# The last token block of a graph layer: multiplication beside the squares, negated offset, early residual loads and two store queues

## The chip, the cores and the metric

One core of one Trainium2 chip. The metric is the device time of one execution in microseconds (us), smaller is better. All numbers below are from executions on the chip.

## The reference, cut to what matters

```python
# x: (128, 64, 768) float32, adj: (128, 64, 64); two layers l of the same form
h = maximum(layernorm(x), 0)
for l in range(2):
    ...                                              # attention from h, W_left, W_right and adj
    h_lin = einsum('bsh,oh->bso', h, W_lin[l]) + b_lin[l]
    ctx = matmul(attention, h_lin)
    h = relu((ctx - mean(ctx)) / (std(ctx) + 0.001) * ln_a[l] + ln_b[l])
return x + h
```

The change touches only the last token block of the last pass: there h_lin is projected, ctx is multiplied, its rows are normalised, scaled by a, shifted by b, clipped at zero, and added to x. In the inputs used here a is all ones and b is all zeros, but the kernel is written for any a and b.

## The kernel before

The 8192 rows are worked through in 16 blocks u of 512 rows. Each block has two halves r, and each half two tiles k of 128 x 768. In the last block (u = 15) the halves are projected one after the other, in fifteen steps of four matmuls each; `run(n)` carries out what was planned with `put(n, ...)` for a place n in that stream. After a projection step the result is read out of PSUM into `hl` by ScalarE and VectorE ("eviction"). When all parts of a half are there, `context` multiplies, and `finish` normalises:

```python
def residual(u, r):                       # asks for the x rows of one half
    XS[u, r] = [sp.tile([P, H], F32, name="xr", bufs=4) for _ in range(2)]
    for k in range(2):
        for h in range(PAIR):
            nc.sync.dma_start(XS[u, r][k][h * S:(h + 1) * S], x[u * NBB + batch(r, k, h)])

def finish(u, r):
    cx = context(u, r)                    # TensorE: two tiles in PSUM
    zs = [sp.tile([P, H], F32, name="z", bufs=4 if last else 3) for _ in range(2)]
    # ... ss, sd, rs
    for k in range(2):                    # ScalarE: sums of squares
        nc.scalar.activation(zs[k].rearrange(two, n=2), cx[k], AF.Square, accum_out=ss[:, k:k + 1])
    nc.scalar.activation(sd, ss, AF.Sqrt, bias=floor, scale=1.0 / (H - 1.0))

    def inverse():
        nc.vector.tensor_scalar_add(rs, sd, EPS_LN)
        nc.vector.reciprocal(rs, rs)

    def scaled(k):
        # ... (last layer)
        nc.vector.scalar_tensor_tensor(zs[k].rearrange(two, n=2), cx[k], rs[:, k:k + 1],
                                       rows["a"].rearrange(two, n=2), op0=ALU.mult, op1=ALU.mult)
        nc.gpsimd.tensor_add(zs[k], zs[k], rows["b"])
        # ...

    def done(k):
        # ... (last layer)
        xs = XS[u, r]
        nc.vector.scalar_tensor_tensor(xs[k], zs[k], 0.0, xs[k], op0=ALU.max, op1=ALU.add)
        for h in range(PAIR):
            nc.sync.dma_start(out[u * NBB + batch(r, k, h)], xs[k][h * S:(h + 1) * S])
        if k and (u < NB - 1 or r == 0):
            residual(u + r, 1 - r)        # asks for the rows of a later half
    return [inverse] + [lambda k=k: scaled(k) for k in range(2)] + [lambda k=k: done(k) for k in range(2)]

# ... the last block: after projection step i, `finish` of a half is begun,
# and its five pieces (inverse, scaled, scaled, done, done) get these places
linear(u, (0,), 0, {0: ((u - 1, 0), (12, 13, 15, 19, 21)),
                    11: ((u - 1, 1), (34, 35, 36, 42, 44))}, (1,))
linear(u, (1,), 30, {4: ((u, 0), (50, 51, 52, 56, 58))}, ())
for n in sorted(plan):
    run(n)
for f in finish(u, 1):
    f()
```

Every engine works off its own instructions in this order. So a piece of `finish` that has to wait holds up all evictions behind it on the same engine: in the profile of this kernel VectorE's addition of (15,0) waits 1.85 us for its rows, and the eviction of Z behind it starts at 2775.32, 3.65 us after TensorE was through with Z (2771.67).

Of the kernel before, what the change touches and what calls it, by code (L numbers as in the profile page):

```python
# [10 lines left out]
F32 = mybir.dt.float32  # L11
I32 = mybir.dt.int32
AF = mybir.ActivationFunctionType
ALU = mybir.AluOpType
# [3 lines left out]
def kernel(  # L18
# [24 lines left out]
    nc = tc.nc  # L43
    B, S, H = x.shape
    L = w_lin.shape[0]
    P = 128
    C = H // P
# [3 lines left out]
    PAIR = P // S  # L51
    Q = 4
    T = Q * P
    TH = T // 2
    NB = B * S // T
    assert L == 2 and PAIR == 2 and C == 3 * K2 and TH == D
    EPS_IN, EPS_LN, EPS_ATT = 1e-5, 1e-3, 1e-10
# [4 lines left out]
    big = ctx.enter_context(tc.tile_pool(name="big", bufs=2))  # L62
    stat = ctx.enter_context(tc.tile_pool(name="stat", bufs=4))
# [5 lines left out]
    NBB = T // S  # L69
# [7 lines left out]
    def put(slot, *fs):  # L77
        plan.setdefault(slot, []).extend(fs)
# [129 lines left out]
    floor = const.tile([P, 1], F32, name="floor")  # L208
# [4 lines left out]
    for h in range(PAIR):  # L213
        r = slice(h * S, (h + 1) * S)
# [287 lines left out]
    rows = {}  # L502
# [45 lines left out]
    def pass_two(l, aside):  # L548
        last = l == L - 1
        with tc.tile_pool(name=f"two{l}", bufs=2, reuse_waits="tile") as sp:  # L550
# [8 lines left out]
            def load(u):  # L559
                if (2, l, u) not in HT:  # L560
                    load_h(2, l, u)
                AT[u] = sp.tile([P, Q, S], F32, name="at", bufs=3)
                nc.sync.dma_start(AT[u], ATT[l][u])

            def context(u, r):


                hl, at = HL[u], AT[u]
                lo, hi = slice(0, S), slice(S, P)
                cx = [ps_aux.tile([P, 2, T], F32, name="aux") for _ in range(2)]  # L570
                for n in range(2):
                    for (j, k, i) in ((lo, 0, lo), (hi, 0, hi), (lo, 1, hi), (hi, 1, lo)):
                        q = r + 2 * k
                        m = n if j == lo else 1 - n
                        nc.tensor.matmul(cx[k][i, m, :HH], at[j, q, :], hl[j, q, m * HH:(m + 1) * HH],  # L575
                                         start=True, stop=True)
                return [c[:, :, :HH] for c in cx]

            def batch(r, k, h):
                return 4 * (h if k == 0 else 1 - h) + r + 2 * k  # L580

            XS = {}

            def residual(u, r):
                XS[u, r] = [sp.tile([P, H], F32, name="xr", bufs=4) for _ in range(2)]
                for k in range(2):
# [5 lines that stand above are left out]
                cx = context(u, r)  # L592
                zs = [sp.tile([P, H], F32, name="z", bufs=4 if last else 3) for _ in range(2)]
                if last and not u and not r:
                    residual(u, r)
                two = "p (n d) -> p n d"
                ss = stat.tile([P, 2], F32, name="ss")
                sd = stat.tile([P, 2], F32, name="sd1")
                rs = stat.tile([P, 2], F32, name="rs1")
# [10 lines that stand above are left out]
                    if last:  # L610
                        nc.vector.scalar_tensor_tensor(  # L611
                            zs[k].rearrange(two, n=2), cx[k], rs[:, k:k + 1],
                            rows["a"].rearrange(two, n=2), op0=ALU.mult, op1=ALU.mult)
                        nc.gpsimd.tensor_add(zs[k], zs[k], rows["b"])  # L614
                        return
                    if (u, r, k) == (NB - 1, 1, 1):
                        nc.vector.tensor_scalar_mul(zs[k].rearrange(two, n=2), cx[k], rs[:, k:k + 1])
                    else:
                        nc.scalar.activation(zs[k].rearrange(two, n=2), cx[k], AF.Copy, scale=rs[:, k:k + 1])
                    for h in range(PAIR):  # L620
                        nc.sync.dma_start(ROWS[u][batch(r, k, h)], zs[k][h * S:(h + 1) * S])

                def done(k):
                    if last:
                        xs = XS[u, r]
                        nc.vector.scalar_tensor_tensor(xs[k], zs[k], 0.0, xs[k], op0=ALU.max, op1=ALU.add)
                        for h in range(PAIR):
                            nc.sync.dma_start(out[u * NBB + batch(r, k, h)], xs[k][h * S:(h + 1) * S])
                        if k and (u < NB - 1 or r == 0):
                            residual(u + r, 1 - r)  # L630

                return [inverse] + [lambda k=k: scaled(k) for k in range(2)] + [lambda k=k: done(k) for k in range(2)]
# [33 lines left out]
            for u in range(NB):  # L666
                turn = not last and u >= NB - 2
                if u + 1 < NB:
                    load(u + 1)
                    put_all(9 if u else 15, affine(2, l, u + 1))  # L670
                    put_sums_t((2, l, u + 1), 15 if u else 21, 1, 0)
                    if turn:
                        load_rows(1, 0, sp)
                        put_all(10, transpose_rows(1, 0, sp), 2)
                    if u in aside:
                        aside[u]()
                    ends = {}
                    if u:
                        ends = {0: ((u - 1, 0), (6, 7, 8, 11, 12)), 7: ((u - 1, 1), (20, 21, 22, 30, 30))}
                    linear(u, (0, 1), 0, ends, (0, 1) if u + 2 < NB else (0,))  # L680
                    for n in sorted(plan):
                        plan[n - 30] = plan.pop(n)
                else:
                    if turn:
                        load_h(1, 1, 0)
                        put_all(28, affine(1, 1, 0), 3)
                        put_sums_t((1, 1, 0), 38, 2, 30)
                    linear(u, (0,), 0, {0: ((u - 1, 0), (12, 13, 15, 19, 21)),
                                        11: ((u - 1, 1), (34, 35, 36, 42, 44))}, (1,))
                    linear(u, (1,), 30, {4: ((u, 0), (50, 51, 52, 56, 58))}, ())  # L690
                    for n in sorted(plan):
                        run(n)
                    for f in finish(u, 1):
                        f()

    def one_aside(l):
# [46 lines left out]
```

## Time and profile before

| | before |
|---|---|
| median of 3 runs | 2791.11 us (2790.47 to 2792.8) |
| span of the profiled execution | 2791.6 us (2793.33 as the runs count it, more than any of them) |
| start of the last token block in it | 2740.0 us |
| from there to the first of the last two squares | 37.9 us |
| from the block's start to the end of the last addition | 46.8 us |
| from the block's start to the end of the span | 51.5 us |

I read every trace relative to the **start of the last block**, which is the first of the four matmuls of its first projection step (X). The rows of the page and of the chain are shown in the prediction; the columns of a chain line are start, length, and what filled it; those of a timeline line are start, length, engine, source line, operation, output and inputs with their shapes, count, and in brackets how long the engine had been idle and what ended that.

### The profile page before, as it was taken

To read this page: it belongs to the slowest core of one execution; us is meant where nothing else is said; L and a number is where in the kernel's file an instruction comes from. 1 tells how busy PE (TensorE), PEld (TensorE's weight loads), DVE (VectorE), ACT (ScalarE), POOL (GpSimd) and SP (SyncE) were. 2 spreads that over 40 slices of the span, in tenths; PEclk is the share of its full clock that TensorE was granted. 3 is DMA by queue.
4 is the path that set the end of the run, shared out by engine and by line. 5 is a ranking of instruction groups with operands and counts; after the bars stand their busy time and mean duration, and the time that the engine had idled before them with its cause. 6 is when DMAs were issued, how large, how long until landed. Compare 5 with 4: busy or idle time off the path is not lost.

```text
span 2791.6 us, 46094 instructions
## 1 busy us (share of the span) xinstructions
PE 2751.3 (99%) x18712; PEld 2340.8 (84%) x18712; DVE 1340.8 (48%) x2215; ACT 837.8 (30%) x1453; POOL 1191.5 (43%) x935
## 2 busy tenths in 40 slices
PE   7999999999999999999999999999999999999997
PEld 6888888888888888888788888888888888888885
DVE  6455545454444332332345444544444335666666
ACT  2122222222231244444521211222121214445443
POOL 3332343223322456556432344223222325887875
PEclk9999999999999999999999999999999999999999
DMA  5533443344332243343555433443344204555654
GB/s 165 152 83 74 108 111 77 74 97 121 79 74 76 84 140 110 113 149 106 149 134 128 116 78 74 97 120 79 74 92 120 62 25 146 167 167 159 184 162 125
DMA packets 234068, 310.80 MB, mean 111 GB/s; under 512 B 54144, under 2 KB 184448, under 8 KB 225664
## 3 DMA queue, kind: packets, MB, share of 16 engines
q1 hardware_dynamic: 233568, 307.06, 41.5%
q8 instruction: 149, 2.44, 0.4%
q10 hardware_dynamic: 288, 0.79, 0.1%
q14 instruction: 63, 0.52, 0.1%
HBM read 202.91 MB, written 104.86 MB: 110 GB/s over the span
## 4 chain that ended last, share of the span: by engine, by line
PE 95%; issue 1%; DVE 1%; POOL 1%; DMA 1%; ACT 1%; SPq 0%; DVEq 0%; ACTq 0%; POOLq 0%
PE X L369 23%; PE V L369 15%; PE X L648 12%; PE Y L369 12%; PE Z L369 8%; PE V L648 8%; PE Y L648 6%; PE aux L395 5%; PE Z L648 4%; PE aux L575 3%; POOL w_r L145 1%; DVE wm L409 0%; DMA x<-in_x_dram 0%; DMA w_r<-in_w_right_dram 0%; DMA w_l<-in_w_left_dram 0%
## 5 line engine op out<-in xcount | busy, mean ns | idle before, releaser
L145 POOL TENSOR_TENSOR ts<-ht 128x512 f32<-128x512 f32 x441 | 586.4, 1341 | 1232.2 <-DMA ht<-h 567.6
L190 ACT ACTIVATE m<-X 128x512 f32<-128x512 f32 x256 | 152.5, 596 | 1106.7 <-PE X L369 582.4
L145 POOL TENSOR_TENSOR ts<-ht,ts 128x512 f32<-128x512 f32 x189 | 249.3, 1327 | 154.7 <-PE X L648 76.9
L145 DVE TENSOR_TENSOR m<-m,V 128x512 f32<-128x512 f32 x256 | 174.2, 680 | 269.5 <-PE V L369 269.4
L145 DVE TENSOR_TENSOR m<-m,X 128x512 f32<-128x512 f32 x256 | 163.7, 681 | 248.7 <-PE X L369 248.0
L369 PE MATMUL X<-ts,w_l 128*128 128x256 f32 x1024 | 244.7, 382 | 3.8 <-DVE w_l L145 2.1
L648 PE MATMUL X<-w_n,ts 128*128 128x256 f32 x1024 | 244.0, 380 | 0.8 <-ACT hl L190 0.6
L369 PE MATMUL X<-ts,w_r 128*128 128x256 f32 x1024 | 241.9, 379 | 0.0
L145 DVE TENSOR_TENSOR m<-m,Z 128x512 f32<-128x512 f32 x128 | 87.9, 687 | 313.4 <-ACT m L190 254.8
L369 PEld LDWEIGHTS X<-ts,w_l 128*128 128x128 f32 x1024 | 193.0, 191 | 35.5 <-DVE m L145 3.1
L648 PEld LDWEIGHTS X<-w_n,ts 128*128 128x128 f32 x1024 | 191.7, 190 | 31.7 <-DVE hl L145 1.8
L369 PEld LDWEIGHTS X<-ts,w_r 128*128 128x128 f32 x1024 | 192.3, 190 | 28.7
L256 ACT ACTIVATE ht<-ht,b_col,a_col 128x512 f32<-128x512 f32 x192 | 143.5, 804 | 142.6 <-DMA ht<-h 142.6
L648 PE MATMUL Y<-w_n,ts 128*128 128x256 f32 x768 | 182.4, 379 | 0.0
L369 PE MATMUL Y<-ts,w_l 128*128 128x256 f32 x768 | 181.4, 379 | 0.0
L369 PE MATMUL Y<-ts,w_r 128*128 128x256 f32 x768 | 181.4, 379 | 0.0
L190 ACT ACTIVATE hl<-X 128x512 f32<-128x512 f32 (+1 forms) x136 | 77.8, 572 | 329.2 <-PE X L648 326.3
L369 PEld LDWEIGHTS Y<-ts,w_r 128*128 128x128 f32 x768 | 145.9, 190 | 19.8
L369 PEld LDWEIGHTS Y<-ts,w_l 128*128 128x128 f32 x768 | 145.9, 190 | 19.8
L648 PEld LDWEIGHTS Y<-w_n,ts 128*128 128x128 f32 x768 | 145.9, 190 | 19.8
L614 POOL TENSOR_TENSOR z<-z,b 128x768 f32<-128x768 f32 x64 | 115.7, 1822 | 94.4 <-DVE z L611 94.4
L145 DVE TENSOR_TENSOR hl<-hl,X 128x512 f32<-128x512 f32 (+1 forms) x136 | 83.1, 652 | 146.6 <-PE X L648 141.8
(106 smaller groups left out, 4682.7 us busy)
## 6 DMA issues: line engine op xcount, KB each, us to landing
ht<-h SPq DMA_DIRECT2D x63, 1536.0 KB, 7.3
h<-xb SPq DMA_DIRECT2D x124, 384.0 KB, 6.4
z<-z SPq DMA_DIRECT2D x128, 192.0 KB, 2.9
x<-z SPq DMA_DIRECT2D x128, 192.0 KB, 8.5
xr<-in_x_dram SPq DMA_DIRECT2D x128, 192.0 KB, 3.7
out_dram<-xr SPq DMA_DIRECT2D x128, 192.0 KB, 2.6
x<-in_x_dram SPq DMA_DIRECT2D x120, 192.0 KB, 8.7
adj<-in_adj_dram SPq DMA_DIRECT2D x64, 128.0 KB, 2.7
```

The costliest lines, as they stand in the source:

```text
L145: (eng.tensor_add if sign == "+" else eng.tensor_sub)(o, a, b)
L190: nc.scalar.activation(to(o), p, AF.Copy, scale=1.0 if sign == "+" else -1.0)
L256: nc.scalar.activation(ht, ht, AF.Relu, bias=cols[1][:, c:c + 1], scale=cols[0][:, c:c + 1])
L369: nc.tensor.matmul(p[:, g], w[ORDER[i][0]][:, c, g * P:(g + 1) * P], b()[t][:, c, :], start=(new and g == c == 0), stop=(c == K2 - 1), ski ...
L395: nc.tensor.matmul(p[h * S + e:h * S + e + 32, q, e:e + 96], ht[:, c, b * S + e:b * S + e + 32], mb[:, e:e + 96], start=(c == 0), stop=(c ...
L575: nc.tensor.matmul(cx[k][i, m, :HH], at[j, q, :], hl[j, q, m * HH:(m + 1) * HH], start=True, stop=True)
L614: nc.gpsimd.tensor_add(zs[k], zs[k], rows["b"])
L648: nc.tensor.matmul(p[:, n], b[t][:, c, r * P:(r + 1) * P], w[s][:, c, :], start=(i in FIRST and i not in PRELOAD and n == c == 0), stop=(c ...
```

## The change

The intent: let the end of the kernel run shorter than 50 us without touching TensorE's work.

1. The x rows of the last block are loaded early, in one go, into the place of a block that is free by then ("ht"), instead of into the four shared buffers that only come free as earlier rows are stored.
2. The places of the pieces move: the context of (14,1) and of (15,0) begins two steps earlier, and the additions of (15,0) go behind the last evictions.
3. The last half gets its own code. Clipping with the offset is rewritten: max(z + b, 0) + x = max(z, -b) + (x + b). So -b and x + b can be formed early on GpSimd, and VectorE multiplies ctx by a while ScalarE still forms the squares; after the squares there remain scale-and-max and one addition.
4. The stores of these rows go out on two queues, of SyncE and ScalarE.

```diff
+            def last_block(u):
+                rest = big.tile([P, C, T], F32, name="ht").rearrange("p c t -> p (c t)")
+                rows["-b"] = sp.tile([P, H], F32, name="nb", bufs=1)
+                for r in range(2):
+                    XS[u, r] = [rest[:, n * H:(n + 1) * H] for n in (2 * r, 2 * r + 1)]
+
+                def load(r):
+                    for k in range(2):
+                        for h in range(PAIR):
+                            nc.sync.dma_start(XS[u, r][k][h * S:(h + 1) * S], x[u * NBB + batch(r, k, h)])
+
+                put(1, lambda: load(1))
+                put(6, lambda: nc.gpsimd.tensor_scalar_mul(rows["-b"], rows["b"], -1.0))
+                put(20, lambda: load(0))
+                for xs, slot in zip(XS[u, 1], (22, 40)):
+                    put(slot, lambda xs=xs: nc.gpsimd.tensor_add(xs, xs, rows["b"]))
+
+            def finish_last(u, r):
+                ... (cx, zs, squares, xs, ss, rs)
+                for k in (1, 0):
+                    nc.scalar.activation(squares[:, k].rearrange(two, n=2), cx[k], AF.Square, accum_out=ss[k])
+                    nc.vector.tensor_tensor(zs[1 - k].rearrange(two, n=2), cx[1 - k],
+                                            rows["a"].rearrange(two, n=2), op=ALU.mult)
+                    nc.scalar.activation(rs[k], ss[k], AF.Sqrt, bias=floor, scale=1.0 / (H - 1.0))
+                for k in (1, 0):
+                    nc.vector.tensor_scalar_add(rs[k], rs[k], EPS_LN)
+                    nc.vector.reciprocal(rs[k], rs[k])
+                    nc.vector.scalar_tensor_tensor(zs[k], zs[k], rs[k], rows["-b"], op0=ALU.mult, op1=ALU.max)
+                    nc.vector.tensor_add(xs[k], xs[k], zs[k])
+                    for h, queue in enumerate((nc.sync, nc.scalar)):
+                        queue.dma_start(out[u * NBB + batch(r, k, h)], xs[k][h * S:(h + 1) * S])
+                return []
...
-                        if k and (u < NB - 1 or r == 0):
+                        if k and u + r < NB - 1:
                             residual(u + r, 1 - r)
...
-                    linear(u, (0,), 0, {0: ((u - 1, 0), (12, 13, 15, 19, 21)),
-                                        11: ((u - 1, 1), (34, 35, 36, 42, 44))}, (1,))
-                    linear(u, (1,), 30, {4: ((u, 0), (50, 51, 52, 56, 58))}, ())
+                        ends = ({0: ((u - 1, 0), (12, 13, 15, 19, 21)), 11: ((u - 1, 1), (34, 35, 36, 42, 44))},
+                                {4: ((u, 0), (50, 51, 52, 56, 58))})
+                    else:
+                        last_block(u)
+                        ends = ({0: ((u - 1, 0), (12, 13, 15, 19, 21)), 9: ((u - 1, 1), (28, 29, 30, 39, 41))},
+                                {2: ((u, 0), (44, 45, 47, 61, 62))})
+                    linear(u, (0,), 0, ends[0], (1,))
+                    linear(u, (1,), 30, ends[1], ())
                     for n in sorted(plan):
                         run(n)
-                    for f in finish(u, 1):
+                    for f in (finish_last if last else finish)(u, 1):
                         f()
```

More of the change, by code (lines that the diff above doesn't have):

```diff
@@ L582, in pass_two @@
             XS = {}
+            def last_block(u):
[13 more added lines that the diff above has]
+            def finish_last(u, r):
+                cx = context(u, r)
+                zs = [sp.tile([P, H], F32, name="z", bufs=4) for _ in range(2)]
+                squares = sp.tile([P, Q, H], F32, name="hl", bufs=2)
+                two = "p (n d) -> p n d"
+                xs = XS[u, r]
+                ss = [stat.tile([P, 1], F32, name="ss_e", bufs=2) for _ in range(2)]
+                rs = [stat.tile([P, 1], F32, name="sd_e", bufs=2) for _ in range(2)]
+                for k in (1, 0):
[11 more added lines that the diff above has]
+                return []
             def residual(u, r):
```

## The prediction

In the recorded text, here and in the expectations below, passages on the hardware that no trace or run of this case shows are cut, and the cuts are marked. No term of its sum is among them: 3.4 + 1.9 + 1.0 = 6.3 us, and 2784.8 us, stand as recorded. What it calls the lock is what it read from the trace of the kernel before: two VectorE additions under a GpSimd addition took 2.54 and 2.43 us instead of 0.94 and 0.95, and ended 0.8 us after it. Its 1.4 us are an estimate that lets the sums x + b and the additions run one after the other with these durations.

> **What bounds the kernel now.** I read in this order: the page's busy shares, its chain that ended last, the chain in order of time for the last 30 us, the timeline and the list of waits there, and at last narrow windows of a few tenths of a microsecond, which separate instructions that the timeline merges. Page first:
>
> ```profile
> PE 2751.3 (99%) x18712; PEld 2340.8 (84%) x18712; DVE 1340.8 (48%) x2215; ACT 837.8 (30%) x1453; POOL 1191.5 (43%) x935
> ...
> PE 95%; issue 1%; DVE 1%; POOL 1%; DMA 1%; ACT 1%; SPq 0%; DVEq 0%; ACTq 0%; POOLq 0%
> ```
>
> TensorE sets 95% of the span. The change leaves its matmuls as they are (an instruction listing of both kernels shows the same ones; only two groups of context products move by two places in the last token block). All streams are the same up to that block, which starts near 2740 us. So the change can only touch the last 50 us of 2791, 2% of the time (56 us) is out of reach, and the question is how many single microseconds the end gives back. The chain there:
>
> ```profile
> 2768.33 0.60 SPq L588
> 2768.93 0.04 issue
> 2768.97 3.14 DMA xr<-in_x_dram
> 2772.12 0.33 DVE hl L145
> 2772.45 1.75 issue
> ...
> 2774.30 0.70 DVE xr L626
> ...
> 2775.32 0.41 DVE hl L145
> 2775.73 0.87 DVE xr L626
> 2776.59 0.34 DVE hl L145
> 2776.94 0.04 issue
> 2776.98 0.90 PE aux L575 x7
> ```
>
> The residual rows of the next-to-last half block are only asked for at 2768.33, after the stores of the half before, because four buffers are shared. VectorE works in order: its addition of those rows (L626) stands before the last two evictions of hl, waits 1.9 us for the load, and so the last context products start at 2776.98 although the last projection step (V, 2772.50 for 1.13 us) was over at 2773.6. After that comes a tail in which every engine waits for another:
>
> ```profile
> 2777.91 0.81 ACT L601 ACTIVATE z<-aux 128x768 f32<-128x768 f32 x1 [11.31 <-PE aux L575]
> ...
> 2779.63 0.30 ACT L603 ACTIVATE sd<-ss,floor 128x2 f32<-128x2 f32 x1
> 2779.96 0.17 DVE L606 TENSOR_SCALAR rs<-sd 128x2 f32<-128x2 f32 x1 [3.04 <-ACT sd L603]
> 2780.16 0.17 DVE L607 RECIPROCAL rs<-rs 128x2 f32<-128x2 f32 x1
> 2780.44 1.94 DVE L611 SCALAR_TENSOR_TENSOR z<-aux,rs,a 128x768 f32<-128x768 f32 x2
> 2781.61 3.56 POOL L614 TENSOR_TENSOR z<-z,b 128x768 f32<-128x768 f32 x2 [7.02 <-DVE z L611]
> 2783.44 3.41 DVE L626 SCALAR_TENSOR_TENSOR xr<-z,xr 128x768 f32<-128x768 f32 x2 [1.06 <-POOL z L614]
> 2786.01 2.42 SPq L628 DMA_DIRECT2D out_dram<-xr  x4
> ```
>
> Context products end at 2777.88, the last addition ends at 2786.85, the last of four store issues starts at 2787.9, the span ends at 2791.6. The two additions are not alike: in narrow windows the first takes 2.54 us, the second 0.94.
>
> [...] the 2.54 us addition lies under the second GpSimd addition, and ends 0.8 us after that one; at 2751.09 another takes 2.43 us, with GpSimd busy to 2752.71:
>
> ```profile
> 2749.12 3.59 POOL L614 TENSOR_TENSOR z<-z,b 128x768 f32<-128x768 f32 x2 [2.37 <-DVE z L611]
> ```
>
> Evictions (PSUM and SBUF) stay at 0.41 us under GpSimd. [...] the trace has 0.94 to 0.95 us for such a free scalar_tensor_tensor. [...] Here an issue is 0.5 to 0.6 us on SP[...].
>
> **The change part by part.**
>
> *Residuals of the last block loaded early* (eight loads, same bytes, into the 12 KB of the block before). The first four issue behind the loads that end at 2748.1: about 2748.2 to 2750.7, and land by 2754 (3.7 us each, median); the others by about 2761. The wait of 1.9 us is gone. The additions of the next-to-last half also go behind the last evictions. What stands between the last projection and the last context products is then one eviction: 0.05 + 0.41, and 0.90 for the products.
>
> *Context of half (14,1) and of (15,0) two steps earlier.* Before, the latter took 2.10 us instead of 1.45: its PSUM places were held by the multiplications at 2759.88 to 2761.82. Earlier slots should remove these 0.65 us. In the last step but one TensorE also waited 0.83 us for an eviction.
>
> Without other trouble: 2773.6 less 0.65, 0.83 and a few tenths gives about 2771.8 for the last projection, plus 0.5 + 0.9: context done about 2773.1, against 2777.88.
>
> *Against it: three new GpSimd operations in this block*, one negation of b (idle place near 2747, free) and two sums x + b of 1.8 us, each directly behind pairs of z + b. [...] I followed the two engines in hand-over order with the durations above: the addition at 2751.09 ends 2753.5 as before, then GpSimd takes x + b to 2755.3, so the second addition, 2754.11 before, ends at 2756.1 instead of 2755.0; the V eviction behind it at 2756.8 instead of 2755.7, and the following V step of TensorE starts near 2756.85 instead of 2755.9 (it needs that eviction). The same again near 2763 to 2765: the addition waits to 2764.65, the chain scale-eviction of X is late, and TensorE's X step loses about 0.7 us. Together 1.4 us (an estimate from these durations): context done about 2774.5. Gain up to here 2777.9 - 2774.5 = 3.4 us.
>
> *The last rows.* VectorE first finishes two additions of half (15,0), which move behind the evictions: 2773.5 to 2775.3. Product with a, half 0: 0.97 us (1.94 / 2), to 2776.25; half 1 to 2777.15. ScalarE's first square (0.81 + 0.2 + 0.3) ends at 2776.0, the other follows the first product and ends at 2777.6: both hidden. Half 1: + eps 0.2, reciprocal 0.25 to the next start, scale-and-max 0.94, addition 0.95: 2779.45. Half 0 the same, 2.25 us: 2781.65. From context end to last addition: 7.1 us, before 8.97 (2786.85 - 2777.88). Gone are the two GpSimd additions and the locked 1.6 us; added are four VectorE passes of which two lie beside the squares. Gain 1.9 us.
>
> *Stores.* Before, the last issue started 1.05 us after the last addition (queue busy with the other half, then one ahead). After, half 1 is out of the way for 2.2 us, and the last two issue together on SP and ACT: 0.06 us. Gain 1.0. From there to the end 3.65 us, as before (2787.9 to 2791.6).
>
> Sum: 3.4 + 1.9 + 1.0 = 6.3 us; 2781.65 + 0.06 + 3.65 = 2785.3 against 2791.6 in the profile. On the median of 2791.11: **2784.8 us**.
>
> **Rivals.** *A: the lock costs nothing on TensorE* (the sums fall into gaps, because their rows land later or the additions come a little earlier): the 1.4 us come back, 7.8 us in all, 2783.3. For it: several of these meetings are within 0.3 us of not happening. Against: GpSimd has no other work between the pairs, so x + b starts at once. *B: a new wait on the way*: [...] the four added loads at slot 20 stand before stores and before the loads for half (14,1), pushing those from 2756.24 to about 2758.4, landing 2762.7 to 2764.0, close to their use at 2763 to 2765; if these come later, VectorE stalls before evictions as it did before, and some 2 us go: 2787. *C: the end is bound by landing*: the ACT queue issues or lands a store later than SP; the loads at the start show ACT issues of 0.43 us, like SP's 0.40, so at most some tenths. *D: nothing changes, since TensorE bounds*: false for the tail, where it is idle for 14 us.
>
> **Range and chances.** Runs of the kernel before differ by 2.3 us (2790.47 to 2792.8). A less noise gives 2782.5, B plus noise 2787.2. Range **2782.5 to 2787.2**. Faster than 2% would need 56 us of a 50 us stretch: 0.005. Slower by 2% needs a fault in the early part, which does not change: 0.005. Within 2%: 0.99.
>
> **What would show it.** In the new profile: no wait of VectorE on a residual load; last context products within 0.6 us of the last projection step's end, near 2773 to 2774.5; second addition of half (14,0) over 1.5 us long (if 0.95, A holds); both products beside squares; about 7 us from context end to last addition; two last issues at once on two queues; 3.7 us from there. It is wrong if TensorE's steps between 2750 and 2773 lose over 2 us, or if the last rows take over 8.5 us.

## The result, and the profile after

| | before | changed |
|---|---|---|
| median of 4 runs on one chip | 2791.45 us (2790.47 to 2792.8) | 2784.34 us (2782.57 to 2786.34) |
| ratio | 1 | 0.9974 (95%: 0.9957 to 0.9992) |

Ratios, here and below, are the mean time of one kernel's fast runs over the mean of the other's fast runs of the same rounds, so not quite the ratio of the medians. The change saves some 7 us; it is within 2%. The prediction was 2784.8. All outputs are right.

Where the microseconds come from is in the two traces, in us after the start of the last block (2740.01 before, 2739.28 changed):

| | before | changed | gained | predicted gain |
|---|---|---|---|---|
| last projection step starts | 32.49 | 31.61 | | |
| first of the last squares starts (the prediction's "context done") | 37.90 | 34.69 | 3.2 | 3.4 |
| from there to the end of the last addition | 8.94 | 6.50 | 2.4 | 1.9 |
| from there to the end of the span | 4.70 | 4.09 | 0.6 | 1.0 |
| end | 51.55 | 45.29 | 6.3 | 6.3 |

The two spans themselves differ by 7.0, of which 0.73 is the start of the last block, in code that did not change.

One row of this table needs care. The first square is not quite the same event in both kernels. Before, tile 0 is squared first, and its products are done before those of tile 1; the changed code squares tile 1 first, whose products come last of all. The timeline of the kernel before has the last ten products and the first square:

```profile
2776.98 1.50 PE L575 MATMUL aux<-hl,at 64*64 64x384 f32 x10 [0.33 <-DVE hl L145]
2777.91 0.81 ACT L601 ACTIVATE z<-aux 128x768 f32<-128x768 f32 x1 [11.31 <-PE aux L575]
```

The square starts 0.6 us before the products end at 2778.48. Counted to the end of *all* products (ends of matmuls are modelled in the trace, so to a tenth or so), the context is done 38.5 us after the block's start before and 34.6 us after it in the changed kernel (2771.84 + 2.08 in the timeline below): gained 3.8, and the rows after it gain 1.8. The sum is the same.

The page of the changed kernel, its row of busy times:

```profile
PE 2747.9 (99%) x18712; PEld 2339.5 (84%) x18712; DVE 1341.2 (48%) x2219; ACT 837.9 (30%) x1454; POOL 1193.9 (43%) x936
```

TensorE has the same 18712 matmuls. The chain of waits of the changed kernel at its end:

```profile
2771.05 0.88 PE V L691 x4
...
2771.95 0.07 DVE hl L145
...
2772.29 1.82 DVE ht L669 x2
2774.11 1.75 DVE z L615 x2
...
2776.15 1.03 DVE z L621
...
2777.20 0.96 DVE ht L622
```

The waits of VectorE on a load and on GpSimd are gone from the chain: behind the last projection step (V) VectorE works almost without a gap through one eviction (L145), the two additions of (15,0) (L669), two products with a (L615), and twice scale-and-max (L621) and addition (L622). The last context products are not in this chain any more, they lie beside the additions. Rows of VectorE, GpSimd, TensorE and ScalarE in the changed kernel's last block, put in order of time; others between them are left out:

```profile
2753.38 0.95 DVE L669 SCALAR_TENSOR_TENSOR xr<-z,xr 128x768 f32<-128x768 f32 x1
2753.79 2.21 POOL L601 TENSOR_TENSOR ht<-ht,b 128x768 f32<-128x768 f32 x1 [1.81 <-DMA ht<-in_x_dram]
...
2761.30 1.81 POOL L601 TENSOR_TENSOR ht<-ht,b 128x768 f32<-128x768 f32 x1
2763.13 0.96 DVE L669 SCALAR_TENSOR_TENSOR xr<-z,xr 128x768 f32<-128x768 f32 x1 [1.27 <-POOL ht L601]
2767.33 1.13 PE L691 MATMUL X<-w_n,ts 128*128 128x256 f32 x4 [0.82 <-DVE hl L145]
...
2771.84 2.08 PE L575 MATMUL aux<-hl,at 64*64 64x384 f32 x16
...
2773.96 0.81 ACT L614 ACTIVATE hl<-aux 128x768 f32<-128x768 f32 x1 [8.76 <-PE aux L575]
2774.03 1.83 DVE L615 TENSOR_TENSOR z<-aux,a 128x768 f32<-128x768 f32 x2
```

To be seen here: of the two meetings of x + b with an addition that I had predicted, the first did not cost TensorE anything in this execution: the addition at 2753.38 is 0.95 us long, because x + b started 0.4 us after it, having waited 1.81 us for its rows; it was x + b that was held up (2.21 us instead of 1.81). The second did: at 2763.13 the addition starts as x + b ends, and TensorE's X step waits 0.82 us. The first square (2773.96) and the first product (2774.03) start together: the one as the context products end, the other as VectorE is through with the two additions.

The DMA issues of the changed kernel from 2778.1 on, with KB of all and us from issue to landing:

```profile
out_dram<-ht SPq DMA_DIRECT2D x2, 192.0 KB, 2.7
out_dram<-ht ACTq DMA_DIRECT2D x2, 192.0 KB, 3.2
```

### The profile page after: what moved, and what is told of

Its sections match the earlier page's. It is cut to its first block, busy times and chain, and to the rows that moved or that the text cites. A ratio compares the mean times of both kernels' runs of the same rounds, so it can differ in the third digit from the quotient of the medians.

```text
span 2784.6 us, 46089 instructions
## 1 busy us (share of the span) xinstructions
PE 2747.9 (99%) x18712; PEld 2339.5 (84%) x18712; DVE 1341.2 (48%) x2219; ACT 837.9 (30%) x1454; POOL 1193.9 (43%) x936
## 4 chain that ended last, share of the span: by engine, by line
PE 96%; DVE 1%; issue 1%; POOL 1%; DMA 1%; ACT 1%; SPq 0%; ACTq 0%; DVEq 0%; POOLq 0%
PE X L369 23%; PE V L369 15%; PE X L691 12%; PE Y L369 12%; PE Z L369 8%; PE V L691 8%; PE Y L691 6%; PE aux L395 5%; PE Z L691 4%; PE aux L575 3%; POOL w_r L145 1%; DVE wm L409 0%; DMA x<-in_x_dram 0%; DMA w_r<-in_w_right_dram 0%; DMA w_l<-in_w_left_dram 0%
## 5 line engine op out<-in xcount | busy, mean ns | idle before, releaser
L145 POOL TENSOR_TENSOR ts<-ht 128x512 f32<-128x512 f32 x441 | 586.4, 1341 | 1232.6 <-DMA ht<-h 607.5
L145 POOL TENSOR_TENSOR ts<-ht,ts 128x512 f32<-128x512 f32 x189 | 249.3, 1327 | 154.7 <-PE X L691 76.9
L145 DVE TENSOR_TENSOR m<-m,V 128x512 f32<-128x512 f32 x256 | 174.2, 680 | 269.6 <-PE V L369 269.5
L145 DVE TENSOR_TENSOR m<-m,X 128x512 f32<-128x512 f32 x256 | 163.7, 680 | 248.9 <-PE X L369 248.2
L145 DVE TENSOR_TENSOR m<-m,Z 128x512 f32<-128x512 f32 x128 | 88.0, 687 | 312.1 <-ACT m L190 253.4
L145 DVE TENSOR_TENSOR hl<-hl,X 128x512 f32<-128x512 f32 (+1 forms) x136 | 83.1, 652 | 145.8 <-PE X L691 140.9
L145 DVE TENSOR_TENSOR hl<-hl,V 128x512 f32<-128x512 f32 (+1 forms) x136 | 89.1, 655 | 128.1 <-PE V L691 127.7
```

The lines of the kernel that those rows point to most:

```text
L145: (eng.tensor_add if sign == "+" else eng.tensor_sub)(o, a, b)
```

## The experiments

All twelve: five rounds each. Kernels are compared only within the same rounds. All differences from the kernel before lie within 2%; an interval that includes 1 shows no difference at all. Edits are relative to the changed kernel.

| run | what | median us (range) | ratio to before (95%) | block end in the trace |
|---|---|---|---|---|
| e1_one_queue | all last stores on one queue | 2784.83 (2784.04 to 2786.83) | 0.9977 (0.9965 to 0.9990) | 45.23 |
| e2_old_rows | early loads and new places, old last rows | 2787.98 (2785.79 to 2789.44) | 0.9985 (0.9972 to 0.9999) | 47.71 |
| e3_old_slots | early loads and new last rows, old places | 2789.83 (2786.53 to 2791.97) | 0.9993 (0.9981 to 1.0006) | 51.28 |
| e4_no_sums | without x + b | 2784.95 (2784.09 to 2786.17) | 0.9977 (0.9965 to 0.9990) | 45.29 |
| e5_load_later | loads for (15,0) behind those for (14,1) | 2784.15 (2782.35 to 2787.07) | 0.9976 (0.9962 to 0.9989) | 46.72 |
| e6_both | e4 and e5 | 2783.72 (2782.04 to 2783.95) | 0.9974 (0.9961 to 0.9986) | 44.51 |
| e7_old_load | e3 without the early loads of (15,0) | 2789.03 (2787.82 to 2792.93) | 0.9996 (0.9984 to 1.0009) | 51.94 |
| e8_sum_later | e5, and the second x + b later | 2782.51 (2782.18 to 2784.85) | 0.9972 (0.9960 to 0.9985) | 44.57 |
| e10_loads_only | early loads alone | 2789.99 (2788.59 to 2790.60) | 0.9997 (0.9984 to 1.0010) | 52.46 |
| e3b_again | e3 once more | 2788.68 (2787.82 to 2791.38) | 0.9993 (0.9979 to 1.0006) | 51.26 |
| e0_again | the changed kernel, unedited | 2782.97 (2781.29 to 2783.72) | 0.9972 (0.9960 to 0.9985) | 46.50 |
| e9_split | e8, + eps on ScalarE, last tile in two column halves | 2782.00 (2780.35 to 2782.91) | 0.9968 (0.9956 to 0.9981) | 43.91 |

The runs tell apart what differs by some 3 us or more. What is below that, I read from the traces, one profiled execution each, against the start of the last block (before: 51.55, changed: 45.29). In e3, e3b, e5, e7, e8 and e10 the profiled execution was the slowest of the five.

### Are two store queues worth anything?

```diff
-                    for h, queue in enumerate((nc.sync, nc.scalar)):
+                    for h, queue in enumerate((nc.sync, nc.sync)):
```

> The changed kernel with the stores of the last half on SP alone. Theory[...]: the last issue starts 0.55 to 0.65 us after the last addition instead of 0.03, the landing stays 2.9 to 3.2 us, so the stretch from the last addition to the end grows from 4.1 to 4.7 us; whole time about 0.6 us above the changed kernel's 2784.3, inside its noise. Rival (two stores started at once on two queues slow each other, which ate the gain: landing was 2.85 us before the change and 3.2 after): with one queue the landing falls back to 2.85 us and the stretch grows only to 4.3 or 4.4 us.

Measured: the last addition ends at 41.19 as in the changed kernel. The last issue is then 0.54 us later instead of 0.03, as the theory says, but the end comes 4.04 us after the addition, against 4.09 with two queues: sooner than the theory (4.7) and the rival (4.3 to 4.4) had it. The DMA issues of this kernel in the same stretch:

```profile
out_dram<-ht SPq DMA_DIRECT2D x4, 192.0 KB, 2.6
```

With one queue a store lands 2.6 us after its issue; with two, that of SyncE's queue 2.7 and that of ScalarE's 3.2. The half microsecond saved at the issue is lost again at the landing: the last store lands 44.39 us after the block's start with one queue and 44.38 with two. Why the stores of two queues take longer to land is not shown. The second queue gains nothing here.

### What do the last rows gain alone?

```diff
-                rows["-b"] = ...
-                put(6, lambda: nc.gpsimd.tensor_scalar_mul(rows["-b"], rows["b"], -1.0))
-                for xs, slot in zip(XS[u, 1], (22, 40)):
-                    put(slot, lambda xs=xs: nc.gpsimd.tensor_add(xs, xs, rows["b"]))
...
-                    for f in (finish_last if last else finish)(u, 1):
+                    for f in finish(u, 1):
```

> Early loads and early slots as in the changed kernel, but the last half block by the old sequence (squares, then scale, b on GpSimd, max and residual), no sums x + b, no negated b, one queue. Theory: the context products come as early as in the changed kernel or up to 1 us earlier (no sums on GpSimd), 33.7 to 34.7 us after the start of the last block, and the rest takes as long as in the kernel before: 13.7 us from the end of the context products to the end of the span. From the start of the block to the end 47.4 to 48.4 us (before 51.5, changed 45.3); whole time 2786.5 to 2787.5. Rival (the old sequence lost its time to the load of the last residuals, not to its own passes): the rest falls to 11 us or less.

Measured: 8.94 us from the first square to the last addition (the kernel before has 8.94 too), then 4.69 to the end (before 4.70, changed 4.09). The last projection step starts at 31.51, as in the changed kernel (31.61), and the last addition ends at 43.02 against 41.19. So the new last rows give 1.8 us in the rows and 0.6 after them, 2.4 in all (47.71 against 45.29), and the early loads with the new places give the other 3.8 of the change's 6.3. That the three GpSimd operations are gone brings the projection only 0.1 us: why, e4 to e6 show. By the runs this kernel lies 3.2 us above e1, which has the new rows.

### Do the early loads need the new places? (e3, e7, e10, e3b)

e3 keeps everything but the old places:

```diff
-                        ends = ({0: ((u - 1, 0), (12, 13, 15, 19, 21)), 9: ((u - 1, 1), (28, 29, 30, 39, 41))},
-                                {2: ((u, 0), (44, 45, 47, 61, 62))})
+                        ends = ({0: ((u - 1, 0), (12, 13, 15, 19, 21)), 11: ((u - 1, 1), (34, 35, 36, 42, 44))},
+                                {4: ((u, 0), (50, 51, 52, 56, 58))})
```

> The changed kernel with the slots of the kernel before: context products of (14,1) and (15,0) two steps later, additions of (15,0) ahead of the last evictions. Theory: the loads are there early, so VectorE does not wait for them, but the context products of (15,0) wait for PSUM again (2.10 us instead of 1.45) and the two additions of 0.95 us push the last evictions: context products end 35.5 to 36.5 us after the start of the last block, against 34.7 in the changed kernel and 37.9 before; the last rows then start sooner after them, since VectorE has no additions left: from the start of the block to the end 45.5 to 46.5 us. Rival (the slots are the larger part, the loads little): 48 us or more.

Measured: 51.28 where 45.5 to 46.5 was expected, and 2789.8 by the runs: in the trace nearly all of the gain is gone, although the load wait is gone too. The last rows are as fast as in the changed kernel (6.50 from the first square), so all is lost before: all context products are done at 40.7, against 34.6 in the changed kernel and 38.5 before. The timeline of e3:

```profile
2772.60 2.54 DVE L669 SCALAR_TENSOR_TENSOR ht<-z,ht 128x768 f32<-128x768 f32 x1 [0.41 <-POOL z L657]
...
2776.73 2.82 PE L575 MATMUL aux<-hl,at 64*64 64x384 f32 x10 [0.34 <-DVE hl L145]
```

Two things. First, the addition of (15,0) no longer waits for its rows, but it now starts beside GpSimd's z + b and takes 2.54 us instead of 0.95; the evictions stand behind it. Second, the last ten context products take 2.82 us; the same ten took 1.50 us in the kernel before (its timeline is shown above).

e7 takes the early loads of (15,0) out of e3 as well, so that the new rows remain, with the early loads and the sums x + b that belong to them:

```diff
(e3, and)
-                put(20, lambda: load(0))
...
-                        if k and u + r < NB - 1:
+                        if k and u < NB - 1:
```

> The new sequence for the last rows, with their residuals early in the free block, but the residuals of (15,0) loaded as in the kernel before and all slots as before. Theory: VectorE waits again 1.5 to 2 us for the residual load of (15,0) ahead of the last evictions, context products end 37.5 to 38 us after the start of the last block as before (37.9); then the new rows take some 2 us less and the stores 1 us less: 47.5 to 48.5 us from the start of the block to the end (before 51.5, changed 45.3); whole time 2787 to 2788. Rival (the gain of the change is nearly all in the last rows): 46 us or less.

Measured: 51.94 where 47.5 to 48.5 was expected. The last projection step starts only at 34.50 (32.49 before, 33.36 in e3), and the first square at 41.35. The 2.0 us by which that step is later than before do not come from the load: both sums x + b ran ahead of an addition here (which then took 2.12 and 2.32 us), and TensorE waited 0.96 and 0.90 us for the evictions behind them. In its timeline the addition waits for the load again, as before:

```profile
2775.31 1.30 DVE L668 SCALAR_TENSOR_TENSOR xr<-z,xr 128x768 f32<-128x768 f32 x1 [1.65 <-DMA xr<-in_x_dram]
```

e10 is another corner, the early loads alone (e2 with the old places, that is, the kernel before with its rows loaded early):

> The kernel before with the early loads of the last block's residuals alone (old slots, old last rows, one queue, no sums). The prediction took the load's wait of 1.9 us as a cost that goes away. Theory formed from the run with the old slots: the wait only changes its name. Without the load the first addition of (15,0) would start when its GpSimd addition ends, 32.8 us after the start of the block, at the same moment as the second GpSimd addition, [...] so it lasts about 2.5 us and ends 35.4 us after the start, as before. Context products then end 37.9 us after the start and the whole is 51.3 to 51.6 us, no gain. Rival (the prediction's first part: the loads are worth the 1.9 us): context products at 36 us, whole 49.6.

Measured: 52.46 in the trace and 2789.99 by the runs, no gain. Its timeline:

```profile
2769.19 2.54 DVE L665 SCALAR_TENSOR_TENSOR ht<-z,ht 128x768 f32<-128x768 f32 x1 [0.41 <-POOL z L653]
2771.99 0.94 DVE L665 SCALAR_TENSOR_TENSOR ht<-z,ht 128x768 f32<-128x768 f32 x1
2772.12 3.75 PE L575 MATMUL aux<-hl,at 64*64 64x384 f32 x14 [1.36 <-DVE hl L145]
```

This block starts at 2736.36, so the context products resume at 2772.12 - 2736.36 = 35.76 us. In the kernel before they resume at 2775.78, which is 35.77 us after its start. The wait of 1.85 us for the load has been replaced by an addition that is 1.6 us longer under GpSimd. What e10 does gain is the second wait, of 0.33 us, as both evictions are now ready. With the new places, where the additions no longer stand before the last evictions, e2 ends 3.84 us earlier than before. The corner that would part the two, **the new places without the early loads, was not run**, so what share of the 3.84 us is of the loads is not shown. It may be small: in the kernel before, the rows of the second tile of (15,0) land 34.96 us after the block's start, so additions behind the evictions would end near 36.1 (an estimate: 34.96, 0.2 until the start, 0.95), about when e2's VectorE goes on to the last rows (36.13).

Then why does e10 start its first square later than before (38.62 against 37.90), although the products resume at the same time? The fourteen products in one go take 3.75 us, against 2.4 (0.86 + 1.50) before. At full clock e10 would end near 51.1, an estimate from these numbers. The view by stretches of time has these columns: stretch, its length, busy time and count of PE, PEld, DVE, ACT and POOL, the granted clock, DMA share, GB/s. For e10:

```profile
2768.64:2772.05 3.41, 1.92 (x6) 0.86 (x6) 3.00 (x4) 0.00 (x0) 2.28 (x2) 1.00 0.00 0
2772.05:2775.47 3.42, 3.35 (x14) 1.12 (x14) 1.21 (x3) 0.50 (x1) 0.00 (x0) 0.50 0.72 184
```

For the kernel before, the stretch that holds its last wait and last context products:

```profile
2774.37:2777.78 3.41, 1.71 (x14) 0.64 (x14) 2.56 (x4) 0.00 (x0) 0.21 (x1) 1.00 0.35 87
```

In e10 the granted clock drops to half (0.50) at 2772.05, just as the last context products begin; the kernel before ran them at full clock (1.00). It is back at 1.00 at 2775.47, 3.42 us later, in e10 and 3.41 us after its step in e7. I had not foreseen this, so e3 was run once more, with its first profile's finding as the expectation:

> The run with old slots again. There the last context products ran at half the granted clock (0.84 to 0.90 us each instead of 0.48 to 0.53), from 37.9 us after the start of the block; this lengthened them from 0.9 to 2.8 us. Theory: [...] if this profile has full clock there, the context products end 38.8 us after the start, and the whole is 49.4 us; if half again, 51.3. In both cases the last evictions come 3.2 us later than in the changed kernel, since the first addition of (15,0) takes 2.5 us under GpSimd; that part must repeat.

Measured: 51.26; the addition takes 2.54 us again, and the half clock sets in again, at 2774.24 (2776.76 in e3, 2776.49 in e7), each time at or shortly before the last products. So all four profiles of kernels with the old places and part of the change were hit. By how much: ten products in 2.82 us against 1.50 before, 1.3 us. At full clock e3 would end near 50.0, an estimate from these two numbers: it would gain 1.6 us rather than 0.3. The runs fit this but do not show it: in all four cases the profiled execution was the slowest of its five, and the medians of e3, e3b and e7 lie 1.5, 1.4 and 1.9 us below the kernel before (e10: 0.1), with intervals that all include 1. The rest that e3 loses against the changed kernel is the late projection (33.36 against 31.61) and the additions before the evictions.

What comes before the step does not tell the cases apart. In the 3.41 us ahead of it TensorE was busy for 1.92 us in e10, e7 and e3b and for 1.71 us in e3, with a longest wait of 1.36 us in all four. But the kernel before had 1.71 us busy in the stretch shown, also with a wait of 1.36 us, and a clock of 1.00 in the next one; the changed kernel had 1.00 after a stretch with 1.76 us busy (2772.17 to 2775.58), and 0.50 only after the following one, which had no matmul at all. And earlier in the block e0_again and e5 waited 1.51 and 1.72 us at one step (below) and kept a clock of 1.00. What brings the half clock is **not settled**; nor is whether the kernel before meets it in some of its executions. It would then be some 1.3 us longer there, and part of the gain of the change in the runs would be this. Of the profiles with the new places, the clock was read for the changed kernel, e2, e5, e8 and e9: it is 1.00 until the context products end. There TensorE goes from the last projection step into the products without such a wait (2771.84 in the changed kernel, 2770.95 in e2), and the sixteen products take 2.08 or 2.09 us.

### What is lost at the X step?

The changed kernel's X step waited 0.82 us (timeline above), at an addition that began when x + b ended. But the residual rows of (14,1) landed at almost the same time, near 2763.0, since the loads for (15,0) were asked for ahead of them. That was my rival B. A two by two experiment: without the sums (e4), with the loads for (15,0) behind those for (14,1) (e5), and both (e6). e4 and e6 give right results only because b is zero here; they are probes, not versions.

```diff
e4 -                for xs, slot in zip(XS[u, 1], (22, 40)):
e4 -                    put(slot, lambda xs=xs: nc.gpsimd.tensor_add(xs, xs, rows["b"]))
e5 -                put(20, lambda: load(0))
e5 +                put(23, lambda: load(0))
e6 = e4 and e5
```

> The changed kernel without the two sums x + b on GpSimd (the offset is left out there; the result is right only because this case's b is zero, and it is meant as a probe). In the changed kernel TensorE loses 1.0 us at its X step, 27.2 us after the start of the block, since VectorE's addition of (14,1) began only when the second sum ended, and, within 0.1 us of it, when the residual load landed. Theory[...]: the loss at the X step falls below 0.3 us and the context products end 33.7 us after the start. Rival B (the load, pushed back by the loads put ahead of it on the same queue): the loss stays at 0.8 to 1.0 us and the products end at 34.5 or later; then VectorE's wait is booked to the load.

> The changed kernel with the four early loads of (15,0) issued behind the loads of (14,1) instead of ahead of them. The loads of (14,1) then issue some 2.5 us sooner. Rival B (the load alone holds VectorE's addition of (14,1)): TensorE's loss of 1.0 us at the X step vanishes, context products end 33.7 us after the start of the last block. Theory[...]: nothing changes, since the second sum still ends at the same place, 23.8 us after the start, and the addition begins there: loss 0.8 to 1.0 us, end at 34.6.

> Both: loads of (15,0) behind those of (14,1), and no sums x + b (probe, right only for zero b). [...] only this run loses the wait: addition of (14,1) starts some 22.6 us after the start of the last block, directly behind the eviction of Y, TensorE's loss at the X step is below 0.3 us, context products end 33.7 us after the start, and the whole is 44.3 us from the start of the block to the end (changed kernel 45.3). If the loss stays, its cause is neither.

Measured, the same addition in the timelines of e4, e5 and e6 in turn:

```profile
2762.61 0.96 DVE L667 SCALAR_TENSOR_TENSOR xr<-z,xr 128x768 f32<-128x768 f32 x1 [1.15 <-DMA xr<-in_x_dram]
```

```profile
2762.66 2.15 DVE L669 SCALAR_TENSOR_TENSOR xr<-z,xr 128x768 f32<-128x768 f32 x1
```

```profile
2759.93 0.95 DVE L667 SCALAR_TENSOR_TENSOR xr<-z,xr 128x768 f32<-128x768 f32 x1
```

Without the sums the same wait stays and is now put down to the load (end 45.29, as before the edit). With the earlier load the addition starts at once but takes 2.15 us beside x + b. Only with both does it start at once and take 0.95; the last projection step starts at 30.85 instead of 31.61, the end is 44.51. So each cause alone was enough for most of the loss (X waited 0.84 us in e4, 0.66 in e5), and taking away either one does not free the step. e5's end of 46.72 has another loss in it, from the first meeting (see below). A profile names one releaser; in the changed kernel the rows landed at 2762.95 and the sum ended at 2763.11.

A version that is right for any b is e5 with the second sum behind the additions of (14,1):

```diff
-                for xs, slot in zip(XS[u, 1], (22, 40)):
+                for xs, slot in zip(XS[u, 1], (22, 48)):
```

> A version that should beat both, if either cause holds the addition of (14,1): loads of (15,0) behind those of (14,1), and the second sum x + b behind the GpSimd additions of (15,0)[...]. Correct for any b. Expected: no loss over 0.3 us at TensorE's X step, context products end 33.7 to 33.9 us after the start of the last block, 44.3 to 44.6 us from the start to the end; whole time 0.7 to 1 us below the changed kernel, inside the noise of the runs. Rival: the second sum, now 1.8 us near the end, meets the two additions of (15,0) behind the last evictions and gives half a microsecond back.

Measured: 44.57, and the last projection step at 30.84, as in e6.

### Is the changed kernel the same in every execution?

No edit; the changed kernel beside three others on another chip.

> The changed kernel once more, as a control on the chip of this call. Expected: 45.3 us from the start of the last block to the end, or up to 1.5 us more if the first sum x + b gets its rows some tenths of a microsecond sooner and then holds VectorE's second addition of (14,0), as it did in the run with the later loads (TensorE's second V step of the first half then lost 1.6 us). Whole time 2783 to 2786.

Measured: 46.50, 1.2 us more than in the first profile. From the timeline of this execution, whose last block starts at 2734.25:

```profile
2748.07 1.80 POOL L601 TENSOR_TENSOR ht<-ht,b 128x768 f32<-128x768 f32 x1 [1.11 <-DMA ht<-in_x_dram]
2748.36 2.33 DVE L669 SCALAR_TENSOR_TENSOR xr<-z,xr 128x768 f32<-128x768 f32 x1
2751.50 1.10 PE L691 MATMUL V<-w_n,ts 128*128 128x256 f32 x4 [1.51 <-DVE hl L145]
```

Here the first meeting took place: GpSimd waited 1.11 us for its rows instead of 1.81 and so began 0.29 us ahead of the addition, which took 2.33 us, and the V step waited 1.51 us. It is a matter of tenths. e5 is of this kind too (wait 1.32 us, addition 2.55, V step waits 1.72), and so is e7 (0.88, 2.12, 0.96). In the profiles of e1, e3, e3b, e8 and e9 GpSimd waited 1.47 us or longer, came second, and the addition took 0.94 or 0.95. So the changed kernel's block takes 45.3 or 46.5 us by when its first rows land; e8 does not remove this.

### A version that beats both?

From e1: there the last issue came 0.54 us after the last addition instead of 0.03, and the end no later (4.04 us after it against 4.09). So make the last store smaller. From the chain: the addition of eps stands on VectorE between the two tiles; ScalarE is idle there. On top of e8:

```diff
+    eps_ln = const.tile([P, 1], F32, name="eps_ln")
+    nc.gpsimd.memset(eps_ln, EPS_LN)
...
                     nc.scalar.activation(rs[k], ss[k], AF.Sqrt, bias=floor, scale=1.0 / (H - 1.0))
+                    nc.scalar.activation(rs[k], rs[k], AF.Identity, bias=eps_ln)
...
-                    nc.vector.tensor_scalar_add(rs[k], rs[k], EPS_LN)
...
-                    nc.vector.tensor_add(xs[k], xs[k], zs[k])
-                    for h, queue in enumerate((nc.sync, nc.scalar)):
-                        queue.dma_start(out[u * NBB + batch(r, k, h)], xs[k][h * S:(h + 1) * S])
+                    for n0, n1 in ((0, H),) if k else ((0, HH), (HH, H)):
+                        nc.vector.tensor_add(xs[k][:, n0:n1], xs[k][:, n0:n1], zs[k][:, n0:n1])
+                        for h, queue in enumerate((nc.sync, nc.scalar)):
+                            queue.dma_start(out[u * NBB + batch(r, k, h)][:, n0:n1], xs[k][h * S:(h + 1) * S, n0:n1])
```

> A version that should beat both: loads of (15,0) behind those of (14,1), second sum behind the GpSimd additions of (15,0), eps added on ScalarE (two small VectorE instructions of 0.15 us and their gaps less), and the last addition in two column halves, each stored at once, so that half of the last 384 KB is under way half a microsecond sooner. Theory (the end is bound by the transfer of the last stores, since one queue and two queues ended at the same 4.05 us after the last addition): last addition 40.2 us after the start of the block (40.5 in the version without these), then 3.5 us to the end: 43.7 to 44.0 us in all. Rival (the landing is a fixed time, whatever its size): 4.0 us after the last addition again, 44.3.

Measured: from the first square to the last addition 6.26 us (6.50 in the changed kernel, 6.56 in e8), from there to the end 3.72 (4.09 in both), block end 43.91. Its DMA issues for the two column halves:

```profile
out_dram<-ht SPq DMA_DIRECT2D x2, 96.0 KB, 2.2
out_dram<-ht ACTq DMA_DIRECT2D x2, 96.0 KB, 2.5
```

Half the bytes land 0.5 and 0.7 us sooner. By the runs e9 has the lowest median of all, 2782.0, and 0.9968 of the kernel before. Against the changed kernel (2782.97) that is 1 us, with ranges that overlap: faster than before is shown, faster than the changed kernel only by the trace.

## Why the prediction was right or wrong

The time was right to half a microsecond: 2784.8 predicted, 2784.34 measured, and the sum of gains, 6.3 us, is that of the traces. The mechanism held in the main, but that it fits so closely is luck: parts that were off by about half a microsecond cancelled, and the changed kernel's own runs spread over 3.8 us. Point by point:

- **TensorE and everything before the last block do not change**: right. Same 18712 matmuls; the block's start differs by 0.7 us between the two profiles, and by up to 5.8 us between all of them, in code that is the same.
- **Early loads remove the wait of 1.9 us**: right for the change as a whole, since the step also moves the additions behind the evictions; 3.8 us of e2 are of loads and places together, and the places were never run alone. By themselves the loads do not do it: in e10 the wait turns into a longer addition beside GpSimd (2.54 us), and TensorE resumes at 35.76 us as at 35.77 before. The half clock that all kernels with part of the change and the old places met in their profiles was no part of my picture.
- **Context of (14,1) and (15,0) two steps earlier**: right. The products of (15,0) take 1.52 us instead of 2.17, and TensorE's wait of 0.83 us is gone; it stood before the last projection step, not before the last but one. Without the meetings the projection is over at 31.86 (e8); without them 31.8 was predicted.
- **Two meetings of x + b with an addition cost 1.4 us**: they do cost time (the addition took 2.15 to 2.55 us instead of 0.95 in e0_again and e5), the size depends on the execution. Against e6 and e8, where TensorE has neither wait, the last projection step comes 31.61 - 30.84 = 0.8 us late in the first profile (one meeting) and 32.84 - 30.84 = 2.0 us in the second (both). The third new GpSimd operation, the negation of b, took 2.13 us, longer than the 1.81 us of a sum that met nothing, but met no addition itself. Rival A held for the first meeting in the first profile. At the second, rival B was there at the same time: the load came as late as the sum, and only taking away both (e6) showed it. So in the first profile the projection was over at 2771.92 - 2739.28 = 32.6 us after the block's start, 0.6 us before the predicted 33.2; in the second it was 0.7 us behind it.
- **Context done 3.4 us earlier**: by the first square 3.2. Two deviations of about 0.6 us cancelled: the projection was 0.6 us early, but the products after it took longer than my 0.90 us. I had taken those from the chain of the kernel before, where they are the seven that the square of tile 0 waited for; the changed code squares tile 1 first and needs all ten (1.50). I did not ask what the new order in the diff means for the first square, and missed this.
- **Last rows**: the mechanism and the size are right. The end of the context is not what the end hangs on, VectorE's own sequence is: from the end of the last projection step to the last addition 8.45 us were predicted (2781.65 - 2773.2) and 8.55 measured (41.19 - 32.64). The sum has a slip: its own terms (1.94 for the products, then twice 0.2 + 0.25 + 0.94 + 0.95) lead from 2775.3 to 2781.9, not to 2781.65; the two passes took 4.69 us, 4.68 by the terms and 4.50 as summed. (In rival A, too, 6.3 + 1.4 is 7.7, not 7.8.) The single terms: two additions 1.82, two products 1.83, scale-and-max 1.02 (0.94 assumed), addition 0.96. That the table shows 2.4 instead of 1.9 is the shifted event; counted to all products it is 1.8. Crossing square and product left both at their length, 0.81 and 0.92 us each.
- **Stores gain 1.0 us, "From there to the end 3.65 us, as before"**: this step failed in size. The issue came 0.03 us after the addition, as predicted, but the end 4.06 us after the issue; gained were 0.6 us. e1 shows that the second queue has no part in it: with one, the end is 4.04 us after the addition. What remains is that the other tile's stores were issued earlier and are out of the way: the first of the last two stores is issued 0.03 us after the addition in e1, 0.36 in e2. I had named the mechanism as rival C and taken it for a few tenths; it took the whole of what the second queue had saved.

In sum, against the predicted end of 45.3 us after the block's start (2785.3 - 2740.0): the meetings cost 0.6 less, VectorE's sequence took 0.1 more, the stores 0.4 more, so 45.3 measured. The total was better than its parts, and in the second profile, with both meetings, it was 1.2 us worse.

Left open: what the new places give without the early loads, what brings the half clock, and how often the kernel before meets it.

## What to carry to other kernels

When a load is made early so that an in-order engine need not wait, look at what that engine's instruction will then run beside: here (e10) the addition no longer waited 1.85 us, but took 2.54 us beside GpSimd's instead of 0.95, and gave back the whole wait until the instruction itself was moved behind the evictions that TensorE needed. When two causes end within a few tenths of a microsecond of each other, removing either can show nothing; try both together before calling one innocent. At the very end of this kernel a second issuing queue did not make the same bytes land sooner (44.38 us after the block's start against 44.39 with one); smaller last stores did (e9: 96 KB landed 2.2 and 2.5 us after the issue, 192 KB in the changed kernel 2.7 and 3.2).
